# Moving twelve bias additions from GpSimd to VectorE in a four-layer graph network, and reordering the end of its third layer

## The chip, the cores and the metric

The kernel runs on one NeuronCore of a Trainium2 chip. A core has a matrix engine (PE, with PEld for its weight loads), a vector engine (DVE), an activation engine (ACT), a general-purpose engine (POOL, GpSimd) and a synchronising engine (SP) that here only starts DMA transfers. The engines run at the same time and wait for each other through semaphores. The metric is the device time of one execution in microseconds (us), as the median of several runs; lower is better.

## The reference, cut to what matters

Four graph layers follow each other on 512 nodes with 768 features; each adds its input and is normalised. All weights are 768 x 768 (or stacks of such).

```python
x = layernorm(x + L0(x))   # attention, 8 heads, then 1 head:  ... + b2
x = layernorm(x + L1(x))   # typed attention, twice:           ... + b2
x = layernorm(x + L2(x))   # three typed convolutions:         ... + b3
x = layernorm(x + L3(x))   # two plain convolutions:           ... + b2

# L2, one convolution (relu after the first two):
out = x @ root + bias
for r in range(4):                   # edge types
    out += rowscale_r * (C_r @ (x @ W[r]))
# L3: h = relu(A @ (x @ W1) + b1); out = A @ (h @ W2) + b2
```

So the last step of every layer is "input + bias row + aggregated products", and the kernel forms "input + bias row" ahead of time, in the buffer into which the products are then added. There are 16 such additions: four layers times four blocks of 128 nodes.

## The kernel before, in words

**Tiling.** Nodes are four blocks of 128 (NB = 4), features six chunks of 128 (KC = 6) or two halves of 384 (j = 0, 1). A product with a 768 x 768 weight is cut into two "units", one per half of the output columns; there are 78 units in the order of use (the list `weights`, then `units`). To keep float32 accuracy in a fast matrix format, every unit is held as three "forms" (w0, w1, w2) and the node matrix as three forms in the tiles S[0..2] (s): `split_piece` makes a third of a unit's forms with one ACT instruction (L778) and two DVE instructions (L779, L780), 128 x 768 each; `split_nodes` transposes a node block on PE (L792) and writes its three forms with ACT (L797) and DVE (L801, L802). The form buffers hold two units, so the forms of unit u go where unit u - 2 was.

**A product** (`product`) is four groups, one per node block: 12 matmuls with the first two forms (L821, L822), a scaling of the sums in PSUM by ACT (L823), then, one group later, 6 matmuls with the third form (L828) and the evacuation. After each group come a job from the list `between` and a call of `split_piece`. `close_group` issues what is open of the last group.

**Layer 0's end.** The last head's `aggregate` makes six columns of Y: PE L1176, then ACT L1183 and L1186, DVE L1187 and L1189, then the three forms of Y by ACT L1193 and DVE L1194 and L1195. The product `head.second` reads Y, with eight jobs that work out the last attention weights. The tiles xin (the layer's input) are loaded by SP (L1397) into buffers that the last head's rows leave free, and POOL adds the bias row (L1398).

**Layer 2, third convolution** (i = 3). Its input S is written column by column by the second convolution's `agg_columns`: DVE L2049, L2050, ACT L1980, DVE L1981, L1982. The output is summed up in acc (128 x 4 x 768), which is first loaded with layer 2's input (`residual`: SP L1989) and gets the bias row from POOL (L1990). Then come the products with root (two), the eight products with W[r] (c_p), and after each the aggregation of the one before it, `agg_rows`: 8 matmuls (L1931) and a DVE addition into acc (L2040). Sums into acc have no order of their own, except that all come after the load and the bias.

**The end of layer 2.** After the last product, six aggregations are left: blocks 2 and 3 of the first half (`agg_rows(R4 - 1, 0, b)`) and four blocks of the second half (`second(b)`). `norm` is DVE bn_stats (L890) twice, aggregate (L892), ACT square root (L894), DVE reciprocal (L895), and DVE subtract-and-scale (L896). `end2(b)` is norm, a store of the block to x_store[2], and `split_nodes` for layer 3. `end_of` puts end2(0) ahead after second(1); second(3) and the other three ends are jobs of layer 3's first product (d1_p0).

**Layer 3.** Two products with W1 (d_p), aggregation by columns (L1943), two with W2, aggregation into acc (L1931, L2114), norm and the output. Before the second product acc is loaded again from x_store[2] (L1989) and POOL adds the bias (L1990).

**What sets the order of instructions.** The code's order gives each instruction a priority; the framework's planner simulates the engines and gives each free engine the ready instruction with the highest priority, so that an instruction written later can be placed earlier when its engine would stand idle. `ahead(f, ...)` raises the priority by 100 places. On the chip each engine then runs its own list strictly in that order.

Of the kernel before, what the change touches and what calls it, by code (L numbers as in the profile page):

```python
# [8 lines left out]
F32 = mybir.dt.float32  # L9
# [13 lines left out]
P = 128  # L23
# [11 lines left out]
def gnn_stack_kernel(ctx: ExitStack, tc: tile.TileContext, a: dict, out: bass.AP):  # L35
# [121 lines left out]
    cT_store = dram.tile([R4 + 1, P, NB, N], F32, tag="cT", name="cT_store")  # L157
    packed_store = dram.tile([NB, P, N], I32, tag="packed", name="packed_store")
    log3_store = dram.tile([NB, P, R3, N], F32, tag="log3", name="log3_store")
    x_store = dram.tile([3, NB, P, D], F32, tag="x", name="x_store")  # L160
    key_store = dram.tile([R3, H1 * N], F32, tag="key", name="key_store")
    flag = const.tile([1, 1], I32, tag="flag", name="flag")

# [550 lines left out]
    def split_layers():  # L714
# [15 lines left out]
            weights += [a[f"L1_gnn_W{i}"][r] for r in range(R3)]  # L730
        for i in (1, 2, 3):
            these = [a[f"L2_gnn_W{i}"][r] for r in range(R4)]
            these.insert(i == 1, a[f"L2_gnn_root{i}"])
            weights += these
        weights += [a["L3_gnn_W1"], a["L3_gnn_W2"]]
        units = [
# [13 lines left out]
        raw, forms = {}, {}  # L750
        loaded, taken, cut, used = [0], [0], [0], [0]
        only_read = []

        def split_piece():

            if taken[0] == len(stream):
                return
            u, p, is_cut = stream[taken[0]]

            if is_cut and u > used[0]:  # L760
                return
            while loaded[0] < min(taken[0] + AHEAD + 1, len(stream)):
                at = loaded[0]
                v, q, _ = stream[at]
                raw[at] = raws.tile([P, KP, HD], F32, tag="raw", name=f"raw{at}")
                nc.sync.dma_start(raw[at], units[v][:, q * KP : (q + 1) * KP, :])
                loaded[0] += 1
            w = raw.pop(taken[0])
            taken[0] += 1
            if not is_cut:  # L770
                only_read[0](u - LAST0, p, w)
                return
            if p == 0:
                forms[u] = [
                    wforms.tile([P, KC, HD], F32R, tag=f"w{f}", name=f"w{f}_{u}") for f in range(3)
                ]
            hm, lo, df = (t[:, p * KP : (p + 1) * KP, :] for t in forms[u])
            nc.scalar.mul(hm, w, ROUND / SPLIT)  # L778
            nc.vector.scalar_tensor_tensor(lo, hm, -SPLIT, w, op0=ALU.mult, op1=ALU.add)  # L779
            nc.vector.tensor_sub(df, hm, lo)  # L780
            cut[0] += 1
# [50 lines left out]

            open_group.append(rest)

        def product(left, evac, name, between=()):

            w = next_unit()
            for b in range(NB):
                bs = slice(b * P, (b + 1) * P)
                po = bank(f"{name}_{b}")  # L840
                group(
                    po[:, :HD],
                    lambda f, bs=bs: [(left[f][:, k, bs], w[f][:, k, :]) for k in range(KC)],
                    lambda b=b, po=po: evac(b, po),
                )
                for job in between[b : b + 1]:
                    job()
                split_piece()

        def product_columns(left, j, evac, name, between=()):  # L850

# [135 lines left out]
        with (  # L987
# [361 lines left out]
            for i in range(H0):  # L1349
                head.aggregate()  # L1350
                jobs = []
                if i == 0:
                    after.h = [row_tile(f"{after.name}_h{b}") for b in range(NB)]
                    for fill in late:
                        fill()
                    after.project(halves=(1,), late=None)
                elif i + 1 < H0:
                    after = Head(i + 1)
                    more = []
                    if i < 3:  # L1360
                        first = 2 * (i - 1)
                        more = [lambda: None] * 8
                        more[1] = lambda: decode3(first)
                        more[5] = lambda: decode3(first + 1)
                    elif i == 3:
                        more = [
                            lambda: None, check_counts, lambda: degrees(0), lambda: None,
                            lambda: None, lambda: degrees(1),
                        ]
                    elif i == 4:  # L1370
                        more = [lambda: None] * 8
                        more[2], more[5] = lambda: degrees(2), lambda: degrees(3)
                    after.project(more)
                if i + 1 < H0:
                    w = after.w
                    soft = [lambda b=b, w=w: w.soft(b) for b in range(NB)]
                    turn = [lambda b=b, w=w: w.turn(b) for b in range(NB)]
                    jobs = [
                        lambda: None, w.keys, soft[0], soft[1], soft[2],
                        lambda: (soft[3](), turn[0]()), lambda: turn[1](),  # L1380
                        lambda: (turn[2](), turn[3]()),
                    ]
                else:
                    cols = small.tile([P, 2, NB], F32, tag="cols", name="gl_cols")
                    w = Weights(cols, "gl")

                    def last_scores():
                        rows = work.tile([P, N], F32, tag="elu_e", name="gl_rows")[:2, :]
                        early.first_rows(Y)
                        early.last_rows(Y, rows)  # L1390
                        nc.vector.tensor_add(cols, parts, early.columns())

                    brow = row_on_all(work, a["L0_gnn_b2"], "gl_b", "arow")
                    xin = []
                    for b in range(NB):
                        xin.append(row_tile(f"xin0_{b}"))
                        nc.sync.dma_start(xin[b], a["x"][b * P : (b + 1) * P, :])  # L1397
                        nc.gpsimd.tensor_tensor(xin[b], xin[b], brow, op=ALU.add)  # L1398
                    soft = [lambda b=b: w.soft(b, divide=False) for b in range(NB)]
                    turn = [lambda b=b: w.turn(b) for b in range(NB)]  # L1400
                    jobs = [
                        last_scores, w.keys, *soft, lambda: turn[0](),
                        lambda: (turn[1](), turn[2](), turn[3]()),
                    ]
                head.second(jobs)
                close_group()
                if i + 1 < H0:
                    head = after
# [575 lines left out]
        def bias_row(v, name):  # L1984
            return row_on_all(tail, v, name, "brow")

        def residual(x_of, b, brow):

            nc.sync.dma_start(acc[:, b, :], x_of)  # L1989
            nc.gpsimd.tensor_tensor(acc[:, b, :], acc[:, b, :], brow, op=ALU.add)  # L1990

        def end_of(second, end):


            second(0)
            second(1)
            ahead(end, 0)
            second(2)
            return [
                lambda: (second(3), ahead(end, 1)), lambda: ahead(end, 2), lambda: ahead(end, 3)  # L2000
            ]


        for i in (1, 2, 3):
# [7 lines left out]
            if i == 3:  # L2012
                brow = bias_row(a["L2_gnn_b3"], f"{name}_b")
                for b in range(NB):
                    residual(x_store[1, b], b, brow)
            def roots(i=i, name=name):
                for j in range(2):

# [11 lines left out]
                    else:  # L2030
                        product_columns(S, j, keep_columns, f"{name}_root{j}")

            if i > 1:
                roots()
            hs = {}

# [18 lines left out]
            for at, (r, j) in enumerate(order):  # L2055
                h = hs[r, j] = new_h(f"{name}_h{r}_{j}")
                jobs = ()
                if j == 0 and r < 2 or j == 1 and 1 <= r < R4 - 1:
                    to = r if j == 0 else r + 1
                    fetch(to)  # L2060
                    if i == 1:
# [2 lines left out]
                                rdeg_row[:, to, :], rdeg[:, to, :], f"rdeg{to}"  # L2064
                            )
                        ]
                if i == 3 and (r, j) == order[-1]:
                    jobs = [lambda: None, lambda: None, lambda: agg_rows(r, 0, 0), lambda: agg_rows(r, 0, 1)]
                if i == 1 and at == 0:
# [2 lines left out]
                    continue  # L2072
                if i == 1 and at == 1:
                    jobs = first_jobs
                product(S, lambda b, po, h=h: split_h(h, b, po), f"{name}_p{r}_{j}", jobs)
                if i == 1 and at == 1:
                    roots()
                if 0 < at and (i < 3 or at < len(order) - 1):
                    close_group()
# [6 lines left out]
            if i < 3:  # L2086
                agg_columns(*order[-1])
                continue
            agg_rows(R4 - 1, 0, 2)
            agg_rows(R4 - 1, 0, 3)  # L2090

            def end2(b):
                norm(acc[:, b, :], b, "l2")
                nc.sync.dma_start(x_store[2, b], acc[:, b, :])
                split_nodes(acc[:, b, :], b, "c3")

            late_ends = end_of(lambda b: agg_rows(R4 - 1, 1, b), end2)


        cT = new_c("d_cT")  # L2100
        nc.gpsimd.dma_start(cT, cT_store[R4])
        row_on_all_of(dinv_row, dinv, "dinv")
        for i in (1, 2):
            name = f"d{i}"
            hs = {}
            if i == 2:
                brow = bias_row(a["L3_gnn_b2"], f"{name}_b")
                for b in range(NB):
                    residual(x_store[2, b], b, brow)

            def agg(j, b):
                po = aggregate(cT, hs[j], b, f"{name}_a{j}")
                half = acc[:, b, columns_of(j)]
# [4 lines left out]
            for j in range(2):  # L2118
                h = hs[j] = new_h(f"{name}_h{j}")
                jobs = ()  # L2120
                if i == 1 and j == 0:
                    jobs = late_ends
                elif i == 2 and j == 1:
                    jobs = [lambda: None, lambda: None, lambda: agg(0, 0), lambda: agg(0, 1)]
                product(
# [66 lines left out]
```

## Time and profile before

| | us |
|---|---|
| median of three runs | 1650.72 (1647.27 to 1652.73) |
| the profiled execution | 1655.17 |
| its span, first to last instruction | 1653.4 |
| PE busy | 1590.9 (96%) |
| DVE busy | 1203.9 (73%) |
| ACT busy | 785.3 (47%) |
| POOL busy | 57.8 (3%), of it 31.4 for the 16 bias additions (8.3, 8.4, 7.4 and 7.3) |

Everything that the prediction takes from the trace is in microseconds from the span's start. In a timeline row the columns are start, duration, engine, line, operation, what is written and read, shapes and number of instructions; in brackets stands how long the engine stood idle before it, and what ended that. Matmuls overlap, so a row's duration is longer than the distance to the next one. In a table by stretches each engine has its busy time and its number of instructions, and PEclk is the share of the full TensorE clock that was granted. The layers lie at about 0 to 694 (layer 0), to 1047 (layer 1), to 1579 (layer 2) and to the end (layer 3).

### The profile page before, as it was taken

How to read it: one execution, taken by the hardware profiler on the slowest of the kernel's cores; microseconds unless marked ns; L12 is line 12 of the kernel's file. 1: busy time of each engine (PE TensorE's matmuls, PEld its weight loads, DVE VectorE, ACT ScalarE, POOL GpSimd, SP SyncE). 2: the span in 40 equal slices, each digit the busy share in tenths (PEclk: the TensorE clock that was granted, in tenths of full speed). 3: DMA queues.
4: the chain of work that ended last, by engine and by line, in shares of the span. 5: the costliest groups of instructions: out<-in, count | busy, mean ns of one | idle time of the engine just before them, and what ended most of it. 6: DMA issues, size and time to landing. Idle time of an engine off the chain costs nothing.

```text
span 1653.4 us, 21322 instructions
## 1 busy us (share of the span) xinstructions
PE 1590.9 (96%) x8085; PEld 1365.7 (83%) x8085; DVE 1203.9 (73%) x2154; ACT 785.3 (47%) x1350; POOL 57.8 (3%) x76
## 2 busy tenths in 40 slices
PE   5989999999999998999899999999999999999997
PEld 2759788797969786776789986889989998999887
DVE  8978898888979697645785986456665568644684
ACT  5665655654555554333785472343344333333352
POOL 0000000000000001000001000000000002000010
PEclk8999999999999999999999999999999999999999
DMA  3233233223323122232113363323332234332321
GB/s 125 78 121 97 89 105 99 86 90 89 106 78 114 38 87 77 97 112 87 45 40 133 97 193 122 116 79 102 96 105 86 83 102 142 101 93 83 112 77 40
DMA packets 84941, 158.04 MB, mean 96 GB/s; under 512 B 6176, under 2 KB 67992, under 8 KB 83168
## 3 DMA queue, kind: packets, MB, share of 16 engines
q1 hardware_dynamic: 79072, 127.79, 25.1%
q0 software_dynamic: 4544, 25.60, 4.7%
q10 hardware_dynamic: 1216, 3.22, 0.5%
q8 instruction: 65, 1.06, 0.3%
q14 instruction: 44, 0.36, 0.1%
HBM read 139.79 MB, written 16.79 MB: 95 GB/s over the span
## 4 chain that ended last, share of the span: by engine, by line
PE 76%; DVE 14%; ACT 4%; DMA 3%; issue 2%; ACTq 0%; DVEq 0%; SPq 0%
PE g_o L1176 10%; PE c_p L821 6%; PE c_p L822 6%; PE c_p L828 6%; PE c_a L1943 5%; PE r_o L1856 4%; PE g_s L821 3%; PE g_s L822 3%; PE g_s L828 3%; PE g_p L821 3%; PE g_p L822 3%; PE g_p L828 2%; PE c_a L1931 2%; PE r_p L821 2%; PE r_p L822 2%
## 5 line engine op out<-in xcount | busy, mean ns | idle before, releaser
L779 DVE SCALAR_TENSOR_TENSOR w<-w,raw 128x768 fp32r<-128x768 f32 x234 | 226.3, 971 | 115.0 <-ACT w L778 112.6
L778 ACT ACTIVATE w<-raw 128x768 fp32r<-128x768 f32 x234 | 195.5, 840 | 126.5 <-PE c_p L821 35.8
L780 DVE TENSOR_TENSOR w<-w,w 128x768 fp32r<-128x768 f32 x234 | 219.0, 951 | 10.4 <-PE c_root L828 4.4
L821 PE MATMUL c_p<-w,s 128*128 128x384 f32 x576 | 192.8, 335 | 0.0
L822 PE MATMUL c_p<-w,s 128*128 128x384 f32 x576 | 192.4, 334 | 0.0
L1176 PE MATMUL g_o<-wT,g_h 128*128 128x512 f32 x384 | 167.0, 595 | 2.6 <-ACT wT L1132 2.6
L1176 PEld LDWEIGHTS g_o<-wT,g_h 128*128 128x128 f32 x384 | 72.7, 191 | 92.3 <-issue 86.4
L1918 DVE TENSOR_TENSOR c_h_lo<-c_p,c_h_hi 128x384 fp32r<-128x384 f32 x96 | 53.2, 554 | 124.1 <-ACT c_h_hi L1917 124.1
L823 ACT ACTIVATE c_p<-c_p 128x384 f32<-128x384 f32 x96 | 45.5, 474 | 196.0 <-PE c_p L822 195.9
L821 PE MATMUL g_s<-w,y 128*128 128x384 f32 x384 | 131.9, 343 | 3.2 <-ACT y L1193 3.2
L821 PE MATMUL g_p<-w,s 128*128 128x384 f32 x384 | 135.0, 351 | 0.0
L822 PE MATMUL g_s<-w,y 128*128 128x384 f32 x384 | 129.3, 337 | 1.0 <-DVE y L1194 1.0
L822 PE MATMUL g_p<-w,s 128*128 128x384 f32 x384 | 130.1, 339 | 0.1
L828 PE MATMUL c_p<-w,s 128*128 128x384 f32 x576 | 117.5, 338 | 0.0
L822 PEld LDWEIGHTS c_p<-w,s 128*128 128x128 f32 x576 | 108.1, 188 | 0.8
L821 PEld LDWEIGHTS c_p<-w,s 128*128 128x128 f32 x576 | 108.1, 188 | 0.7
L828 PEld LDWEIGHTS c_p<-w,s 128*128 128x128 f32 x576 | 100.2, 188 | 4.1 <-ACT c_p L823 4.0
L828 PE MATMUL g_p<-w,s 128*128 128x384 f32 x384 | 79.3, 340 | 0.4 <-ACT g_p L823 0.3
L828 PE MATMUL g_s<-w,y 128*128 128x384 f32 x384 | 78.7, 340 | 0.3 <-ACT g_s L823 0.3
L821 PEld LDWEIGHTS g_s<-w,y 128*128 128x128 f32 x384 | 72.4, 188 | 4.2 <-ACT y L1193 4.0
L822 PEld LDWEIGHTS g_p<-w,s 128*128 128x128 f32 x384 | 72.6, 189 | 3.2 <-issue 1.9
L821 PEld LDWEIGHTS g_p<-w,s 128*128 128x128 f32 x384 | 72.6, 189 | 3.1 <-issue 2.0
(336 smaller groups left out, 3321.1 us busy)
## 6 DMA issues: line engine op xcount, KB each, us to landing
raw<-in_L_gnn_W_dram SPq DMA_DIRECT2D x222, 384.0 KB
c_cT<-cT_store POOLq DMA_DIRECT2D x12, 1024.0 KB, 5.9
raw<-in_L_gnn_root_dram SPq DMA_DIRECT2D x18, 384.0 KB
r_log<-log_store SPq DMA_DIRECT2D x8, 768.0 KB
cT_store<-r_qk SPq DMA_DIRECT2D x20, 256.0 KB
g_s<-in_L_gnn_a_src_dram POOLq DMA_DIRECT2D x8, 384.0 KB, 4.2
g_d<-in_L_gnn_a_dst_dram POOLq DMA_DIRECT2D x8, 384.0 KB, 4.4
log_store<-z SPq DMA_DIRECT2D x12, 256.0 KB
```

Source lines behind the costliest of these rows:

```text
L778: nc.scalar.mul(hm, w, ROUND / SPLIT)
L779: nc.vector.scalar_tensor_tensor(lo, hm, -SPLIT, w, op0=ALU.mult, op1=ALU.add)
L780: nc.vector.tensor_sub(df, hm, lo)
L821: nc.tensor.matmul(out, l0, r0, start=(k == 0), stop=False)
L822: nc.tensor.matmul(out, l1, r1, start=False, stop=(k == KC - 1))
L823: nc.scalar.mul(out, out, SPLIT + 1.0)
L828: nc.tensor.matmul(out, l2, r2, start=False, stop=(k == KC - 1), skip_group_check=True)
L1176: nc.tensor.matmul(po, self.h[k][:, c * P : (c + 1) * P], wT[:, k, :], start=(k == 0), stop=(k == NB - 1),)
L1856: nc.tensor.matmul(po[:, :n], wT[:, k, :], source(k, at), start=(k == 0), stop=(k == NK - 1),)
L1918: nc.vector.tensor_sub(lo, po[:, :HD], hi)
L1931: nc.tensor.matmul(po[:, :HD], cT[:, k, bs], h[f][:, k, :], start=(k + f == 0), stop=(k == NB - 1 and f == 1),)
L1943: nc.tensor.matmul(po, h[f][:, k, cs], cT[:, k, :], start=(k + f == 0), stop=(k == NB - 1 and f == 1),)
```

## The change

1. Layer 0: the four POOL additions into xin become DVE additions, two in each of the last two jobs of `head.second`.
2. Layer 2, third convolution: the four POOL additions into acc become DVE additions, jobs of the first product. The products with root move behind the first two products with W[0]; the list of weights is changed accordingly.
3. Layer 3: x_store[2], its four stores and four loads go away. The normalised blocks stay in acc, and the bias is added there by DVE, as jobs of the second product with W1.
4. The end of layer 2: the order is now sum, sum, ..., all six aggregations, with the four norms and the transposes of the first two blocks put between or behind them; the transposes of the last two blocks are jobs of layer 3's first product.
5. The last product of layer 2 no longer calls `split_piece` (unit 74, W1's first half, is cut at the start of its own product in the code's order), and unit 75 (W1's second half) first gets a copy of one column of S from the third block into its first form: its forms can't be made before that block's S is written.

The four additions in layer 1 (L1849) stay on POOL.

```diff
-        x_store = dram.tile([3, NB, P, D], ...)
+        x_store = dram.tile([2, NB, P, D], ...)
...
-            these.insert(i == 1, a[f"L2_gnn_root{i}"])
+            these.insert(i != 2, a[f"L2_gnn_root{i}"])
...
+        behind = {len(units) - 3: lambda: S[2][:, KC - 1, 3 * P - 1 : 3 * P]}
...
+            if p == 0 and u in behind:
+                nc.scalar.copy(hm[:, 0, :1], behind[u]())
             nc.scalar.mul(hm, w, ROUND / SPLIT)
...
-        def product(left, evac, name, between=()):
+        def product(left, evac, name, between=(), cuts=True):
...
-                split_piece()
+                if cuts:
+                    split_piece()
...
-                        nc.gpsimd.tensor_tensor(xin[b], xin[b], brow, op=ALU.add)
+                    def bias(*blocks):
+                        for b in blocks:
+                            nc.vector.tensor_add(xin[b], xin[b], brow)
...
-                        last_scores, w.keys, *soft, lambda: turn[0](),
-                        lambda: (turn[1](), turn[2](), turn[3]()),
+                        last_scores, w.keys, *soft, lambda: (turn[0](), bias(0, 1)),
+                        lambda: (turn[1](), turn[2](), turn[3](), bias(2, 3)),
...
-        def residual(x_of, b, brow):
-            nc.sync.dma_start(acc[:, b, :], x_of)
-            nc.gpsimd.tensor_tensor(acc[:, b, :], acc[:, b, :], brow, op=ALU.add)
-        def end_of(second, end):
+        def add_bias(b, brow):
+            nc.vector.tensor_add(acc[:, b, :], acc[:, b, :], brow)
+        def end_of(first, second, rows, turn):
+            first(2)
             second(0)
+            first(3)
             second(1)
-            ahead(end, 0)
+            ahead(rows, 0)
             second(2)
-            return [
-                lambda: (second(3), ahead(end, 1)), lambda: ahead(end, 2), lambda: ahead(end, 3)
-            ]
+            ahead(rows, 1)
+            ahead(second, 3)
+            ahead(turn, 0)
+            ahead(rows, 2)
+            ahead(turn, 1)
+            ahead(rows, 3)
+            return [lambda: ahead(turn, 2), lambda: ahead(turn, 3)]
...
-                    residual(x_store[1, b], b, brow)
+                    nc.sync.dma_start(acc[:, b, :], x_store[1, b])
...
-            if i > 1:
+            if i == 2:
                 roots()
...
+                if i == 3 and at == 0:
+                    jobs = [lambda b=b, brow=brow: add_bias(b, brow) for b in range(NB)]
...
-                product(S, lambda b, po, h=h: split_h(h, b, po), f"{name}_p{r}_{j}", jobs)
-                if i == 1 and at == 1:
+                product(
+                    S, lambda b, po, h=h: split_h(h, b, po), f"{name}_p{r}_{j}", jobs,
+                    cuts=i < 3 or at < len(order) - 1,
+                )
+                if i != 2 and at == 1:
                     roots()
...
-            def end2(b):
-                norm(acc[:, b, :], b, "l2")
-                nc.sync.dma_start(x_store[2, b], acc[:, b, :])
-                split_nodes(acc[:, b, :], b, "c3")
-            late_ends = end_of(lambda b: agg_rows(R4 - 1, 1, b), end2)
+            late_ends = end_of(
+                lambda b: agg_rows(R4 - 1, 0, b), lambda b: agg_rows(R4 - 1, 1, b),
+                lambda b: norm(acc[:, b, :], b, "l2"),
+                lambda b: split_nodes(acc[:, b, :], b, "c3"),
+            )
...
+        brow = bias_row(a["L3_gnn_b2"], "d_b")
...
-            if i == 2:
-                brow = bias_row(a["L3_gnn_b2"], f"{name}_b")
-                for b in range(NB):
-                    residual(x_store[2, b], b, brow)
...
+                elif i == 1:
+                    jobs = [lambda b=b: add_bias(b, brow) for b in range(NB)]
```

More of the change, by code (lines that the diff above doesn't have):

```diff
@@ L159, in gnn_stack_kernel @@
     log3_store = dram.tile([NB, P, R3, N], F32, tag="log3", name="log3_store")
-    x_store = dram.tile([3, NB, P, D], F32, tag="x", name="x_store")
+    x_store = dram.tile([2, NB, P, D], F32, tag="x", name="x_store")
     key_store = dram.tile([R3, H1 * N], F32, tag="key", name="key_store")
@@ L2088, in split_layers @@
                 continue
-            agg_rows(R4 - 1, 0, 2)
-            agg_rows(R4 - 1, 0, 3)
-            def end2(b):
-                norm(acc[:, b, :], b, "l2")
-                nc.sync.dma_start(x_store[2, b], acc[:, b, :])
-                split_nodes(acc[:, b, :], b, "c3")
-            late_ends = end_of(lambda b: agg_rows(R4 - 1, 1, b), end2)
+            late_ends = end_of(
[3 more added lines that the diff above has]
+            )
         cT = new_c("d_cT")
```

## The prediction

> **What bounds the kernel now.** I read the page's busy shares and its chain first: PE is busy for 96% of the span and has 76% of the chain, so an edit elsewhere pays only where PE stands still. Then I listed PE's idle stretches in the timeline. Between 560 and 1653 us, outside layer 1, only three places have idle rows over 0.15 us on PE: layer 0's end, the start of layer 2's third convolution, and layer 2's end. The change touches exactly these.
>
> Layer 0's end, PE, then POOL, then DVE:
>
> ```profile
> 630.04 0.44 PE L822 MATMUL g_s<-w,y 128*128 128x384 f32 x1 [0.75 <-DVE y L1194]
> 635.57 0.44 PE L821 MATMUL g_s<-w,y 128*128 128x384 f32 x1 [3.22 <-ACT y L1193]
> ...
> 627.60 8.25 POOL L1398 TENSOR_TENSOR xin<-xin,gl_b 128x768 f32<-128x768 f32 x4 [42.58 <-DMA xin<-in_x_dram]
> ...
> 624.24 0.68 DVE L1195 SCALAR_TENSOR_TENSOR y<-y,y 128x512 fp32r<-128x512 f32 x1
> 628.36 1.63 DVE L1194 TENSOR_TENSOR y<-g_y,y 128x512 fp32r<-128x512 f32 x1 [1.04 <-ACT y L1193]
> 629.91 2.06 DVE L1187 TENSOR_SCALAR g_e<-g_e 128x512 f32<-128x512 f32 x1
> 631.89 2.29 DVE L1195 SCALAR_TENSOR_TENSOR y<-y,y 128x512 fp32r<-128x512 f32 x1
> ```
>
> While POOL adds, three DVE instructions take 1.63, 2.06 and 2.29 us; the same lines take 0.69, 0.42 and 0.68 just before. PE waits behind them. The start of the third convolution shows the same: two S forms at 1.75 and 2.37 instead of 0.68, each beside a POOL addition.
>
> ```profile
> 1389.57 2.06 POOL L1990 TENSOR_TENSOR acc<-acc,c_b 128x768 f32<-128x768 f32 x1 [0.46 <-DMA acc<-x_store]
> ...
> 1390.42 1.75 DVE L1981 SCALAR_TENSOR_TENSOR s<-acc,s 128x512 fp32r<-128x512 f32 x1
> 1392.70 2.37 DVE L1982 SCALAR_TENSOR_TENSOR s<-s,s 128x512 fp32r<-128x512 f32 x1
> ...
> 1396.32 0.79 PE L822 MATMUL c_root<-w,s 128*128 128x384 f32 x3 [1.14 <-DVE s L1981]
> ```
>
> Layer 2's end: PE waits for the norms, DVE is full (11.77 of 12.00 us in 1553 to 1565), and weight forms stand between the norms.
>
> ```profile
> 1561.67 1.19 PE L792 MATMUL c_t<-ident,acc 128*128 128x128 f32 x6 [3.04 <-DVE acc L896]
> 1578.83 0.84 PE L792 MATMUL c_t<-ident,acc 128*128 128x128 f32 x6 [1.56 <-DVE acc L896]
> ...
> 1559.60 0.90 DVE L779 SCALAR_TENSOR_TENSOR w<-w,raw 128x768 fp32r<-128x768 f32 x1
> 1576.59 2.09 DVE L896 TENSOR_SCALAR acc<-acc,l_mv,l_rstd 128x768 f32<-128x768 f32 x1
> ...
> 1549.46 0.85 ACT L778 ACTIVATE w<-raw 128x768 fp32r<-128x768 f32 x1 [2.82 <-PE c_p L821]
> ...
> 636.00:642.00 6.00, 5.31 (x20) 2.60 (x18) 1.52 (x3) 1.49 (x3) 0.00 (x0) 0.72 0.00 0
> 1562.00:1582.00 20.00, 18.02 (x103) 16.98 (x101) 16.14 (x31) 7.11 (x17) 5.55 (x3) 0.91 0.45 155
> ```
>
> The last two rows are stretches: the granted clock is 0.72 and 0.91 right behind the two long waits. After 3.04 us of idle time the matmuls at 1562.5 come every 0.32 us instead of 0.173. So a long wait costs its length and a slow stretch after it.
>
> **Layer 0's end.** Idle: 0.75 + 3.22 + 0.22 + 0.33 = 4.5 us. Slow stretch, by the distances of matmuls at full clock: 12 matmuls in 1.11, 2.26 and 0.83 us instead of 0.52, 1.37 and 0.52, so 1.8. Ceiling 6.3. Without POOL the three DVE instructions lose 0.94 + 1.64 + 1.62 = 4.2 us, so the last column's forms come 4.2 us earlier, at about 631.4 and 632.2. PE then has its 8 matmuls of 0.25 us up to 631.2 and waits some 0.2 twice: no slow stretch. The four additions on DVE cost 0.87 each, by L780, which has the same shape, both inputs in SBUF, and that distance: 3.5 us. They are written into the last jobs, 655 to 666, where DVE is busy 18.4 of 25 us and PE is never idle: free there. But they are ready when the loads land, near 628 to 635, and the planner may put one into a pause of DVE on the chain (there are two, of 1.0 and 0.7 us). All four there would cost 3.5 and leave 0.7. I take **5.0** (between 0.7 and 6.3, near the top since whatever else waits on DVE has the higher priority).
>
> **Start of the third convolution.** PE needs 10.3 us for the 59 matmuls between 1388.12 and 1400.65 and takes 12.5: 2.25 lost. The two slow forms cost DVE 1.07 + 1.69 = 2.8 us, which is more, so nearly all goes. Worst: all four additions (3.5) between S's columns, 0.7 slower than now. DVE's list is full up to 1399 with work of higher priority, so I take **1.8** (-0.7 to 2.25). Behind it, four DVE additions may stand waiting for loads that land as late as 1402.2; queued behind them are forms of the product after next and evacuations, both a product (12.5 us) early: nothing. Moving root by two products adds no PE instruction, and the h tiles that then wait longest are not needed earlier: nothing; its other side is a stall of DVE of at most those 3 us, under the same 12.5.
>
> **Layer 2's end.** Between 1558.30 and 1582.54 PE has 80 matmuls and 28 transposes, 16.9 us at full distances, and takes 24.2: 7.3 lost, of it 5.0 idle (3.04, 0.41, 1.56) and 2.3 slow. After the change all six sums stand before the first transposes: 6 x 1.39 us from 1552.9, up to 1561.2. The first norm needs its sum (done by 1557.1 at the latest), then 2.7 us of DVE and ACT: ready at 1559.8, before PE has run out. What is late next is DVE: from 1553.3 it has six additions (3.1), seven bn_stats (3.3), norms (2.8), two blocks of S forms (3.8) and an h form (0.5), so 13.5 us, until about 1566.7, while PE wants the second block's forms near 1565.5. With unit 75's six instructions (5.2 us) still in between, that would be 5 us later; this is what the copy prevents. I leave 2.5 us of waits, with no slow stretch: gain **4.8** (top 7.3). The held forms become due at about 1576, when PE starts W1's second half; DVE can begin them at 1569.7, behind 1.9 us for the fourth block and 1.5 for h forms, so the first pieces are there and the last comes about on time. The copy itself is one small ACT instruction, nearest row L894 (128x1, 0.29 us), with scalings (L823) queued behind it; between 0 and 1 us, inside the 2.5.
>
> **Layer 3.** Four stores and four loads go from SP's queue; nobody on PE waits for them. The load of layer 3's bias row (0.55 on POOL) is written earlier, behind the load of its matrix; POOL has nothing else queued until the end, and now it runs at 1405, some 170 us early: nothing. Root's weight loads swap places with W[0]'s in SP's list, as many and as large: nothing. POOL's additions at 1568 to 1588 go, and with them the two slow norms (1.55 and 2.09 against 0.67), already counted. The four DVE additions (3.5) fall into 1577 to 1597, where DVE has 14.7 of 20 us and PE is dense; should they slip into the columns after it (DVE 14.56 of 16) they delay S by up to 0.9 each. I take **-0.4** (0 to -3.5).
>
> Sum: 5.0 + 1.8 + 4.8 - 0.4 = **11.2 us** off the profiled execution's 1655.17 (span 1653.4 and 1.8 around it), so 1644.0. The median shown is 4.45 lower; the edits have nothing to do with that difference, so the forecast is 1650.72 - 11.2 = **1639.5**.
>
> The Trainium skill speaks against a part of this. "TensorE: Matmul & The Clock Gate", in Part 1, has the clock halved only after an idle window of about 3.4 us. By it neither wait here (3.04, 3.22) would bring a slow stretch, and 4.1 us of the ceilings would not exist: about 7 us instead of 11.2. The rows of 0.72 and 0.91 show that they did.
>
> **Rivals.** (a) *One site does not pay*: the xin additions land in the chain of Y, leaving 0.7 of 5.0, or DVE remains the bound at layer 2's end, leaving about 0.5 of 4.8. Sum near 6.9, time 1644 (1642 to 1647.5). For it: DVE is full there whatever POOL does. Against: the weight forms leave. 20%. (b) *No change*: POOL isn't the cause of the slow instructions, or PE's waits only move; 1650. Against it: every slow instruction lies beside a POOL addition, in all three places. 11%. (c) *Slower*: W1's forms come too late. Unit 74 is no longer cut in the last product but behind the norms in priority. If its six DVE instructions (5.2 us) really come after 1553, DVE has 16.2 + 5.2 us until 1574.5 before layer 3's first group can end; PE is out of work at 1564.5, idles 10 us, runs 2.3 slow, and with layer 3's four additions (3.5) in the same queue and 1 us for unit 75 loses 16.8 instead of 7.3. That is 9.5 worse against 6.8 gained elsewhere: 1653.5. It decides when the three ACT instructions of unit 74 start after 1553. Against it: now they start at 1529.82, as soon as the buffer is free and 8 us ahead of their place in the code, as do those of every unit before it. 9%.
>
> **Numbers.** The main case has 60%: 1634.8 (all ceilings) to 1642. About 0.3% (5 us) is what a measurement of this kernel can tell from no change, so faster means under 1645.8: all of the main case and 13 of (a)'s 20 points, 73%. Within: 7 of (a), 10 of (b), 1 of (c), 18%. Slower: 8 of (c), 1 of (b). The range from 1634 to 1650 holds the main case, (a) and half of (b).
>
> **What would show it.** Right: in the changed trace L1194, L1187 and L1195 take 0.4 to 0.7 us at 627 to 632 and PE idles under 1 us there; no S form over 1 us at the third convolution's start; the last sum before the first L792 of layer 3, idle time before that under 1 us; L778 of unit 75 after 1565; granted clock 1.00 in both stretches. Wrong: DVE additions within the chain of Y, or PE idle ahead of W1's products.

## The result and the profile after

The changed kernel takes 1640.90 us (median of 7 runs, 1638.24 to 1642.83); the kernel before, on the same chip, 1650.72 (7 runs, 1646.32 to 1652.73). The ratio is 0.9942, 95% interval 0.993 to 0.9953. The forecast of 1639.5 was 1.4 us low. The profiled execution took 1640.9 us with a span of 1639.1. One execution in experiment 9 took 2282.56 us at a mean granted clock of 0.66 and is left out of that experiment's ratio.

In the changed file the prediction's lines have moved. L1187, L1189, L1193, L1194 and L1195 are now L1194, L1196, L1200, L1201 and L1202; L778 to L780 are L783 to L785; L792 is L797; L821, L822, L823 and L828 are L826, L827, L828 and L833; L896 is L903; L1931 is L1942; L1981, L1982, L2040 and L2049 are L1992, L1993, L2058 and L2067. New are the additions (L1408 in layer 0, L2000 in layers 2 and 3) and the copy (L782). In the kernels of experiments 2, 3 and 11 some lines move on by one to six more.

I cut both traces at the same instructions and compared the stages. Outside the three places all engines have the same lists of instructions.

| stage, cut at | before | after | difference |
|---|---|---|---|
| start, to the issue of the bias row gl_b | 584.49 | 583.29 | -1.20, same list |
| layer 0's end, to layer 1's first load on POOL | 110.77 | 105.20 | -5.57 |
| layer 1 | 352.12 | 350.11 | -2.01, same list |
| layer 2's first two convolutions | 341.19 | 341.22 | +0.03, same list |
| third convolution's first relation | 76.57 | 74.32 | -2.25 |
| its other relations | 72.95 | 73.01 | +0.06, same list |
| layer 2's end, to layer 3's first aggregation | 57.63 | 54.21 | -3.42 |
| the rest | 57.68 | 57.74 | +0.06 |

The touched stages gained 11.2 us. The spans differ by 14.3 because untouched code was 3.1 faster in this one execution; the medians differ by 9.8.

**Layer 0's end after**, timeline of DVE and PE, then one stretch (columns: stretch, its length, busy time of PE, PEld, DVE, ACT and POOL, granted clock, DMA):

```profile
626.38 0.96 DVE L1408 TENSOR_TENSOR xin<-xin,gl_b 128x768 f32<-128x768 f32 x1 [0.26 <-DMA xin<-in_x_dram]
627.26 0.68 DVE L1201 TENSOR_TENSOR y<-g_y,y 128x512 fp32r<-128x512 f32 x1
627.86 0.42 DVE L1194 TENSOR_SCALAR g_e<-g_e 128x512 f32<-128x512 f32 x1
628.20 0.68 DVE L1202 SCALAR_TENSOR_TENSOR y<-y,y 128x512 fp32r<-128x512 f32 x1
...
632.07 0.80 PE L833 MATMUL g_s<-w,y 128*128 128x384 f32 x3 [0.34 <-ACT g_s L828]
...
632.00:638.00 6.00, 5.79 (x33) 4.56 (x34) 2.06 (x4) 1.39 (x4) 0.00 (x0) 1.00 0.01 3
```

The three slow instructions are at 0.68, 0.42 and 0.68 us. PE's waits for Y (0.75, 3.22 and 0.22 us) are gone; the 0.34 us left are the wait for ACT's scaling that was there before (0.33). The clock stays at 1.00 where it was 0.72. One of the new additions stands at 626.38, in the middle of Y's chain; the other three followed at 629.46, 630.93 and 632.40.

**The third convolution's start after**, DVE, then the stretch:

```profile
1385.87 0.94 DVE L2000 TENSOR_TENSOR acc<-acc,c_b 128x768 f32<-128x768 f32 x1
1386.73 0.68 DVE L1992 SCALAR_TENSOR_TENSOR s<-acc,s 128x512 fp32r<-128x512 f32 x1
...
1388.20 0.68 DVE L1993 SCALAR_TENSOR_TENSOR s<-s,s 128x512 fp32r<-128x512 f32 x1
...
1386.00:1398.00 12.00, 11.99 (x69) 11.66 (x68) 11.61 (x16) 6.95 (x15) 0.54 (x1) 1.00 0.45 130
```

The S forms take 0.68 us although additions stand between them, and PE is busy for 11.99 of 12 us. In the 12.53 us from 1379.37, which match the prediction's 1388.12 to 1400.65, it is busy for 12.52 us (10.90 before).

**Layer 2's end after**, PE, then ACT, then stretches:

```profile
1550.32 0.82 PE L797 MATMUL c_t<-ident,acc 128*128 128x128 f32 x6
1553.30 1.54 PE L797 MATMUL c_t<-ident,acc 128*128 128x128 f32 x6 [2.17 <-DVE acc L903]
...
1538.52 0.85 ACT L783 ACTIVATE w<-raw 128x768 fp32r<-128x768 f32 x1 [2.82 <-PE c_p L826]
1539.69 0.82 ACT L783 ACTIVATE w<-raw 128x768 fp32r<-128x768 f32 x1
1560.28 0.18 ACT L782 CAST w<-s 128x1 fp32r<-128x1 f32 x1
1562.18 0.84 ACT L783 ACTIVATE w<-raw 128x768 fp32r<-128x768 f32 x1
...
1552.00:1558.00 6.00, 4.70 (x24) 4.63 (x25) 5.66 (x16) 2.96 (x7) 0.00 (x0) 0.72 0.00 0
1562.00:1582.00 20.00, 20.00 (x116) 19.70 (x115) 14.71 (x19) 10.52 (x19) 0.00 (x0) 1.00 0.25 79
```

All six sums now stand ahead of the first transposes, which start at 1550.32 without a wait. The second block's transposes still wait 2.17 us for their norm, and the six transposes take 1.54 us instead of 0.82: a slow stretch. From 1562 on PE is full (20.00 of 20). The ACT rows hold the surprise. The copy (1560.28) and the form behind it (1562.18) came late as wanted, but two thirds of unit 75 (1538.52, 1539.69) went ahead of the norms all the same. The copy is written for p == 0 alone, and it touches one column of the first third; the other two thirds depend on nothing.

### The profile page after: what moved, and what is told of

Its sections match the earlier page's. It is cut to its first block, busy times and chain, and to the rows that moved or that the text cites. A ratio compares the mean times of both kernels' runs of the same rounds, so it can differ in the third digit from the quotient of the medians.

```text
span 1639.1 us, 21279 instructions
## 1 busy us (share of the span) xinstructions
PE 1587.8 (97%) x8085; PEld 1366.4 (83%) x8085; DVE 1199.1 (73%) x2166; ACT 785.9 (48%) x1351; POOL 33.7 (2%) x64
## 3 DMA queue, kind: packets, MB, share of 16 engines
q10 hardware_dynamic: 1216, 3.22, 0.5%
## 4 chain that ended last, share of the span: by engine, by line
PE 83%; DVE 10%; ACT 4%; DMA 2%; issue 1%; ACTq 0%; DVEq 0%
PE g_o L1183 10%; PE c_p L833 6%; PE c_p L826 6%; PE c_p L827 6%; PE c_a L1954 5%; PE r_o L1867 4%; PE g_s L826 3%; PE g_s L827 3%; PE g_s L833 3%; PE g_p L826 3%; PE g_p L827 3%; PE r_p L826 3%; PE r_p L827 3%; PE r_p L833 3%; PE g_p L833 3%; PE c_a L1942 2%
## 5 line engine op out<-in xcount | busy, mean ns | idle before, releaser
L784 DVE SCALAR_TENSOR_TENSOR w<-w,raw 128x768 fp32r<-128x768 f32 x234 | 222.0, 953 | 114.3 <-ACT w L783 112.4
L783 ACT ACTIVATE w<-raw 128x768 fp32r<-128x768 f32 x234 | 195.3, 839 | 126.4 <-PE c_p L826 35.9
L785 DVE TENSOR_TENSOR w<-w,w 128x768 fp32r<-128x768 f32 x234 | 218.8, 950 | 10.5 <-PE c_root L833 4.4
L826 PE MATMUL c_p<-w,s 128*128 128x384 f32 x576 | 191.2, 335 | 0.0
L827 PE MATMUL c_p<-w,s 128*128 128x384 f32 x576 | 190.8, 334 | 0.0
L828 ACT ACTIVATE c_p<-c_p 128x384 f32<-128x384 f32 x96 | 45.3, 474 | 191.8 <-PE c_p L827 191.8
L826 PE MATMUL g_p<-w,s 128*128 128x384 f32 x384 | 134.6, 351 | 0.0
L826 PE MATMUL g_s<-w,y 128*128 128x384 f32 x384 | 131.9, 343 | 0.0
L827 PE MATMUL g_p<-w,s 128*128 128x384 f32 x384 | 130.1, 339 | 0.1
L827 PE MATMUL g_s<-w,y 128*128 128x384 f32 x384 | 129.3, 337 | 0.1
L833 PE MATMUL c_p<-w,s 128*128 128x384 f32 x576 | 117.3, 338 | 0.0
L827 PEld LDWEIGHTS c_p<-w,s 128*128 128x128 f32 x576 | 108.0, 188 | 0.8
L826 PEld LDWEIGHTS c_p<-w,s 128*128 128x128 f32 x576 | 108.0, 188 | 0.7
L833 PEld LDWEIGHTS c_p<-w,s 128*128 128x128 f32 x576 | 100.2, 188 | 4.2 <-ACT c_p L828 4.2
L833 PE MATMUL g_p<-w,s 128*128 128x384 f32 x384 | 79.3, 340 | 0.4 <-ACT g_p L828 0.3
L833 PE MATMUL g_s<-w,y 128*128 128x384 f32 x384 | 78.1, 338 | 0.3 <-ACT g_s L828 0.3
L827 PEld LDWEIGHTS g_p<-w,s 128*128 128x128 f32 x384 | 72.6, 189 | 3.1 <-issue 1.9
L1954 PE MATMUL c_a<-c_cT,c_h_lo 128*128 128x512 f32 x192 | 75.1, 391 | 0.0
L1954 PE MATMUL c_a<-c_cT,c_h_hi 128*128 128x512 f32 x192 | 75.1, 391 | 0.0
```

What stands on the lines that cost most here:

```text
L826: nc.tensor.matmul(out, l0, r0, start=(k == 0), stop=False)
L827: nc.tensor.matmul(out, l1, r1, start=False, stop=(k == KC - 1))
L828: nc.scalar.mul(out, out, SPLIT + 1.0)
L833: nc.tensor.matmul(out, l2, r2, start=False, stop=(k == KC - 1), skip_group_check=True)
L1954: nc.tensor.matmul(po, h[f][:, k, cs], cT[:, k, :], start=(k + f == 0), stop=(k == NB - 1 and f == 1),)
```

## The experiments

My theory after reading the traces had three parts. First, DVE instructions are slow only beside POOL's additions, by contention and not by a dependency. Second, layer 2's end gained from POOL, from the order and from the held form, each in part. Third, it gained less than forecast because two thirds of unit 75 were not held. The rivals are in the expectations. Each kernel below is the changed kernel with the edit shown; its stage times stand against the changed kernel's 105.20, 74.32 and 54.21 us.

### 1. Layer 0's additions on POOL again

```diff
-                            nc.vector.tensor_add(xin[b], xin[b], brow)
+                            nc.gpsimd.tensor_tensor(xin[b], xin[b], brow, op=ALU.add)
```

> The changed kernel with one thing undone: layer 0's four additions stand on POOL again, in the old place of the code. Contention theory: DVE's instructions become slow only beside POOL's additions. L1201, L1194 and L1202 beside them take 1.6 to 2.3 us again, PE waits 0.8 and 3.2 us, the stretch behind it runs at a granted clock near 0.72, and layer 0's end takes 5.6 us more than in the changed kernel; the other two places stay as in the changed kernel; the time is about 1646.5. Rival, order: the gain came from the additions' place among DVE's instructions or from run-to-run differences in untouched code; then the three instructions keep 0.4 to 0.7 us and layer 0's end takes 0 to 1 us more, time about 1641.

Measured: 1645.76 us (8 runs), ratio to before 0.9967 (0.9957 to 0.9978). Layer 0's end takes 110.36 us, 5.16 more; the other two places are as in the changed kernel (74.32, 54.17). POOL, DVE and PE:

```profile
625.59 1.84 POOL L1408 TENSOR_TENSOR xin<-xin,gl_b 128x768 f32<-128x768 f32 x1 [42.64 <-DMA xin<-in_x_dram]
627.61 6.23 POOL L1408 TENSOR_TENSOR xin<-xin,gl_b 128x768 f32<-128x768 f32 x3 [0.18 <-DMA xin<-in_x_dram]
...
626.28 1.70 DVE L1201 TENSOR_TENSOR y<-g_y,y 128x512 fp32r<-128x512 f32 x1 [1.04 <-ACT y L1200]
627.90 2.06 DVE L1194 TENSOR_SCALAR g_e<-g_e 128x512 f32<-128x512 f32 x1
629.88 2.30 DVE L1202 SCALAR_TENSOR_TENSOR y<-y,y 128x512 fp32r<-128x512 f32 x1
632.10 0.74 DVE L1196 SCALAR_TENSOR_TENSOR g_y<-g_o,bcols,g_e 128x512 f32<-128x512 f32 x1
...
633.55 0.61 PE L826 MATMUL g_s<-w,y 128*128 128x384 f32 x1 [3.22 <-ACT y L1200]
```

The contention theory holds, with almost the old numbers: L1201, L1194 and L1202 take 1.70, 2.06 and 2.30 us, and PE waits 0.82 and 3.22 us; the granted clock from 634 to 640 is 0.74. Read L1201's end: 626.28 + 1.70 = 627.98. POOL's first addition ended at 627.43, 0.55 us earlier. L1196 at 632.10 also lies beside POOL's additions (627.61 to 633.84) and keeps its 0.74; its first input, g_o, comes from PSUM.

### 2 and 3. Work on POOL that nobody waits for

Four extra additions on POOL, each started by the landing of a block of x, and in a second kernel three memsets in the place of each addition:

```diff
+                    spare = work.tile([P, D], F32, tag="arow", name="spare")
+                    for b in range(NB):
+                        nc.gpsimd.tensor_copy(spare[:, :1], xin[b][:, :1])
+                        nc.gpsimd.tensor_tensor(spare, brow, brow, op=ALU.add)
...
+                        for n in range(3):
+                            nc.gpsimd.memset(spare, float(n))
```

> The changed kernel with four extra POOL additions at layer 0's end whose result nobody uses, each with two inputs in SBUF (the bias row added to itself) and started by the landing of a block of x, as the old additions were; the four real additions stay on DVE. Contention theory: nobody waits for POOL's work, yet the DVE instructions beside it take 1.6 to 2.3 us, and layer 0's end is 4 to 5.6 us longer, or more, since the real additions on DVE become slow too. Rival, dependency: Y's chain was late because something waited for POOL's results or its queue; then nothing waits here and the stage is as long as in the changed kernel (0 to 0.3 us).

> The same place and trigger as the run with extra POOL additions, but POOL only writes: three memsets of 128x768 for each block of x, whose result nobody uses. If contention is a matter of POOL's use of SBUF as such, DVE's instructions beside the memsets are slow here as well (1.6 to 2.3 us, stage 3 to 6 us longer). If it takes POOL's reading of two inputs, they keep 0.4 to 0.7 us and the stage is as in the changed kernel (0 to 0.5 us). I expect the second, with 60 in 100.

Measured: with the extra additions layer 0's end takes 109.72 us (+4.52; one run, 1645.29), with the memsets 105.08 (-0.12; one run, 1642.39). POOL and DVE with the extra additions:

```profile
624.34 2.23 POOL L1409 TENSOR_TENSOR spare<-gl_b 128x768 f32<-128x768 f32 x1
627.24 1.54 POOL L1409 TENSOR_TENSOR spare<-gl_b 128x768 f32<-128x768 f32 x1
...
625.16 1.96 DVE L1201 TENSOR_TENSOR y<-g_y,y 128x512 fp32r<-128x512 f32 x1
627.38 1.95 DVE L1202 SCALAR_TENSOR_TENSOR y<-y,y 128x512 fp32r<-128x512 f32 x1
```

With the memsets:

```profile
628.38 2.55 POOL L1410 MEMSET spare<- 128x768 f32 x3
...
629.23 0.69 DVE L1201 TENSOR_TENSOR y<-g_y,y 128x512 fp32r<-128x512 f32 x1
629.84 0.42 DVE L1194 TENSOR_SCALAR g_e<-g_e 128x512 f32<-128x512 f32 x1
```

Nobody reads the spare tile, so nothing waits for the results of the extra additions. One dependency is left: DVE's addition into a block of x waits for POOL's one-column copy out of it (0.50 us before the first of them). The memset kernel has the same copies and loses nothing, so contention is shown. The size tells its kind. L1201 ends at 627.12 and POOL's addition at 626.57, 0.55 earlier; L1202 ends at 629.33 and POOL's next at 628.78, again 0.55. An instruction that takes 0.68 alone has 0.55 left when POOL's ends, whenever it started: it stands still until then. So DVE doesn't run at part speed, it waits. Beside memsets, which read nothing, DVE runs at its full speed.

"SBUF — State Buffer" in the Trainium skill, section "Who interferes with whom", states this as an exclusive lock: a DVE instruction with two SBUF inputs and a GpSimd instruction that reads SBUF can't run together, and the second one blocks fully. The rows agree: five ends at POOL's end plus 0.55 us (one in experiment 1, two here, two in experiment 11), none slow beside memsets.

### 4. No form held back

```diff
-        behind = {len(units) - 3: lambda: S[2][:, KC - 1, 3 * P - 1 : 3 * P]}
+        behind = {}
```

> The changed kernel without the held-back weight forms: no copy, unit 75's first third is made when its buffer is free, as the other two thirds already are in the changed kernel. As the prediction had it, the copy keeps 5.2 us of DVE work out of the norms: without it layer 2's end is 5 us longer, time about 1646. By the trace of the changed kernel only one third is held: 1.7 us of DVE work joins ahead of the norms, of which PE sees between 0 and 1.7 us: time 1641 to 1643. A third reading, that the copy does nothing: 0.

Measured: layer 2's end takes 55.12 us, 0.91 more; 1640.99 us (4 runs), ratio 0.994 (0.9923 to 0.9956), which the time can't tell from the changed kernel. PE waits 2.42 us ahead of the second block's transposes and 0.57 later. The prediction gave the copy 5 us; as written it is worth 0.9.

### 5 and 10. All of unit 75 held back

```diff
-            if p == 0 and u in behind:
+            if u in behind:
```

> The changed kernel with one more thing: the copy that holds a weight form back is written for all three thirds of unit 75, not for the first alone. My theory: in the changed kernel two thirds (3.6 us of DVE work) still go ahead of the norms, and turn 1 waits 2.17 us for its norm; with all of it held, norm 1 comes up to 2.2 us earlier, the wait is under 0.5 us, the clock stays at 1.00, and layer 2's end is 2 to 3.4 us shorter: time 1638 to 1639. Rival: DVE's order of sums, statistics and forms sets norm 1, not the weight forms; then the wait stays and the stage is as before (0 to 0.5 us). Second rival: with 5.2 us of forms behind the norms, W1's second half comes late; then PE waits ahead of its products at about 1573 and the time is 1641 to 1645.

> The changed kernel with all three thirds of unit 75 held back, timed in more rounds. Theory: the wait of turn 1 stays at 0.5 us, too short for a slow stretch, so layer 2's end is 51.8 us in every execution: 0.8 us less than the changed kernel where that one has no slow stretch, 2.4 less where it has one; median 1 to 2.4 us under the changed kernel's, ratio to before near 0.993. Rival: the gain of the profiled execution is given back in untouched code; then the two medians agree within 0.5 us.

Measured: layer 2's end takes 51.81 us in the first trace and 51.82 in the second, 2.4 less than in the changed kernel's profiled execution. Times: 1640.39 us (4 runs), ratio 0.9932 (0.9913 to 0.995), and 1639.95 (6 runs), ratio 0.993 (0.9916 to 0.9945). PE and ACT in the first trace:

```profile
1553.27 0.87 PE L797 MATMUL c_t<-ident,acc 128*128 128x128 f32 x6 [0.50 <-DVE acc L903]
...
1561.81 0.28 ACT L782 CAST w<-s 128x1 fp32r<-128x1 f32 x2 [1.02 <-DVE s L807]
1562.41 1.57 ACT L783 ACTIVATE w<-raw 128x768 fp32r<-128x768 f32 x2
1564.49 0.84 ACT L783 ACTIVATE w<-raw 128x768 fp32r<-128x768 f32 x1
```

Now all three forms start behind 1562, the wait for the norm is 0.50 us, the clock stays at 1.00, and no product of layer 3 waits for unit 75. The theory of the missing two thirds holds for the stage. That it shows in the time is likely, not certain: on the same chip as the second run the changed kernel's median was 1642.68 us, 2.7 more, and its ratio 0.994 (0.9923 to 0.9958), so the intervals overlap.

### 6. The old order at layer 2's end, additions on DVE

```diff
-            ahead(rows, 0)
+            ahead(end, 0)
             second(2)
-            ahead(rows, 1)
...
-            return [lambda: ahead(turn, 2), lambda: ahead(turn, 3)]
+            return [
+                lambda: (second(3), ahead(end, 1)), lambda: ahead(end, 2), lambda: ahead(end, 3)
+            ]
```

(with first(3) ahead of second(0) as before, and no form held back)

> The changed kernel, but at layer 2's end the old order of sums and transposes and no held-back form; layer 3's additions stay on DVE and the additions in place. It splits the gain of this stage (3.4 us) into the part of POOL's additions and the part of the order. Theory: the slow norms beside POOL's additions (1.55 and 2.09 instead of 0.67) were 2.3 us of the old stage, so it is 2 us shorter than before and 1.4 us longer than in the changed kernel, with waits ahead of the transposes of 2 to 3 us each still there: time about 1642. Rival: the order is all of it; then the stage is 3 us or more longer than in the changed kernel, 1644. Second rival: POOL is all of it; 0, 1641.

Measured: 56.54 us, 1.09 less than before and 2.33 more than in the changed kernel; 1642.55 us (4 runs), ratio 0.9947 (0.9928 to 0.9966). PE waits for the first block's norm as long as before the change:

```profile
1549.59 0.87 PE L797 MATMUL c_t<-ident,acc 128*128 128x128 f32 x6 [3.04 <-DVE acc L903]
```

So this stage's 3.42 us are 1.1 for the additions on DVE, in place and without the stores and loads, which no run takes apart (57.63 to 56.54), 1.4 for the order (to 55.12 in experiment 4) and 0.9 for the third that is held (to 54.21). All four kernels have one slow stretch here, so they can be compared. I had put POOL's part at 2.

### 7, 8 and 11. Root's place, cutting in the last product, POOL in the third convolution

```diff
-            these.insert(i != 2, a[f"L2_gnn_root{i}"])
+            these.insert(i == 1, a[f"L2_gnn_root{i}"])
...
-                    cuts=i < 3 or at < len(order) - 1,
+                    cuts=True,
...
                     nc.sync.dma_start(acc[:, b, :], x_store[1, b])
+                    nc.gpsimd.tensor_tensor(acc[:, b, :], acc[:, b, :], brow, op=ALU.add)
```

(three kernels; the first also calls roots() where it was called before, the third drops the DVE jobs)

> The changed kernel with the products of the third convolution's root ahead of the first relation's, as before; the additions stay on DVE. If the start of this convolution gained by POOL's silence alone, the stage behind it is as in the changed kernel (0 to 0.3 us). If the four additions on DVE then stand in the way of S's forms, up to 0.7 us of additions each, the stage is up to 2.8 us longer. I expect 0 to 1 us, since the acc of these additions is needed by root's sums first.

> The changed kernel, but the last product of layer 2 goes on cutting weight forms as before. In the changed kernel unit 74's forms were made in the same stretch as before, so the planner takes them when their buffer is free, wherever the code puts them; I expect 0 (within 0.3 us in layer 2's end). Rival: the order of writing counts for the planner's ties and the stage gets 1 to 3 us longer.

> The changed kernel with the third convolution's four additions on POOL again, right behind the loads of acc; root's products stay behind the first relation's. Contention theory: S forms beside POOL's additions take 1.7 to 2.4 us instead of 0.68, PE waits about 1.1 us and the stage is 1.5 to 2.3 us longer. Rival: what helped is that root's products come later, so that their additions are not due yet; then the S forms are slow or not, but PE doesn't wait: 0 to 0.3 us.

Measured, one run each (1637.82, 1640.41 and 1642.56 us). With root first the third convolution's first relation takes 74.26 us (-0.06): root's place is worth nothing once the additions are on DVE. With cuts=True the stages up to layer 2's end are as they were, and that end takes 52.58 instead of 54.21, with the same wait of 2.17 us and DVE's and ACT's instructions in the same order; experiment 9 shows why. With POOL's additions it takes 76.01 (+1.69), and the S forms are slow:

```profile
1382.23 2.07 POOL L2033 TENSOR_TENSOR acc<-acc,c_b 128x768 f32<-128x768 f32 x1 [0.46 <-DMA acc<-x_store]
...
1382.49 0.69 DVE L2068 TENSOR_TENSOR c_t<-c_a,rdeg_row 128x512 f32<-128x512 f32 x1
1383.09 1.76 DVE L1992 SCALAR_TENSOR_TENSOR s<-acc,s 128x512 fp32r<-128x512 f32 x1
```

L1992 (two inputs in SBUF) ends 0.55 us after POOL's addition: 1384.85 and 1384.30. L2068 (L2067 in the changed kernel), in the same 2 us, has one input in PSUM (c_a) and keeps its 0.69. A second pair is alike: L1992 ends at 1388.33, POOL's next addition at 1387.78. PE waits 0.49 and 0.55 us, where it was 0.48 and 1.14. The old place of root cost the other 0.6 us (76.57 against 76.01), so by these traces, one of each kernel, the place mattered only beside POOL.

### 9. The changed kernel again

> The changed kernel itself once more, on the same chip as the run that holds all of unit 75 back. Turn 1 waits 2.17 us in every trace of this code, and behind it the granted clock is 0.5 for 3.4 us in some traces and 1.00 in others; layer 2's end should be 54.2 us with the slow stretch or 52.6 without, nothing in between. Time 1639 to 1642.

Measured: ratio 0.994 (0.9923 to 0.9958). Its layer 2's end takes 54.19 us. The code of this end is the same, with the same 2.17 us wait, in eight traces of this study (cuts=True included, whose wait is the same). Five have 54.17 to 54.21 us (the changed kernel, 1, 2, 7, 9) and three 52.57 or 52.58 (3, 8, 11). The kernel with memsets has no slow stretch; PE, then the stretch:

```profile
1556.46 0.87 PE L797 MATMUL c_t<-ident,acc 128*128 128x128 f32 x6 [2.17 <-DVE acc L903]
...
1554.00:1560.00 6.00, 3.83 (x31) 3.55 (x30) 6.00 (x16) 3.49 (x9) 0.00 (x0) 1.00 0.00 0
```

Clock 1.00 here, 0.72 in the like stretch of the changed kernel, after an equal wait. One slow stretch costs 1.6 us of this stage.

## Why the prediction was right, point by point

**Layer 0's end: right.** Forecast -5.0 us; measured -5.57, and 5.16 by undoing it alone. The cause was named rightly. One step was wrong without cost: the additions did not run at 655 to 666. (The prediction's 18.4 of 25 us is not DVE's load there, which was 8.14 of 11; about as much, 18.27, lies in 641 to 666.) Three ran inside Y's chain and the fourth right behind it. The prediction had named this as a sign of being wrong and priced it at 3.5 us. Of the 2.6 us of the three, about 1.5 fell into pauses, by an estimate from DVE's idle rows (1.04 and 0.70 us in experiment 1, 0.26 here). The last forms started at 630.33 and 631.79, up to 0.8 us later than forecast when this trace's earlier start is allowed for, and PE waited for neither.

**The third convolution's start: right, small.** Forecast -1.8; measured -2.25, the ceiling. I had kept 0.45 for additions in the way of S. They do stand between S's last columns (1385.87), and PE doesn't notice. The loads came earlier than the 1402.2 that I had allowed for: all four additions are over by 1391.67.

**Layer 2's end: the direction right, a step wrong.** Forecast -4.8; measured -3.42. The step that failed is "with unit 75's six instructions (5.2 us) still in between, that would be 5 us later; this is what the copy prevents". The copy holds two of the six DVE instructions; the four others (3.5 us by the prediction's 0.87 each) ran ahead of the norms. I had read "p == 0" as "before the first piece, hence before all", though a dependency here joins only regions that overlap. Without the copy the stage is 0.9 us longer, not 5; with all three thirds held it is 2.4 shorter, in all 5.8 less than before. So all six instructions in between cost 3.3 us (51.81 to 55.12), a slow stretch included, and the 5 us were too much as well. "No slow stretch" failed with it: the wait left was 2.17 us, and 1.6 us of the stage hangs on the clock behind it. That DVE would be late next was right; it was late with the second block's norm, not with its S forms. The changed kernel without a slow stretch (52.6, -5.1) would have met the forecast, by luck.

**Layer 3 and the rest: right.** Forecast +0.4; measured +0.06. The additions run on DVE at 1565 to 1576 beside a full PE. The third rival (W1's forms late, slower) did not occur: unit 74's ACT instructions start at 1518.88, 8.3 us ahead of the stage's start, exactly as before (1529.82), and they do so with cuts=True too (experiment 8).

**The sum.** 11.2 us were forecast, and the three stages gave 11.2 in the profiled executions, partly by errors that cancel: 0.6 and 0.45 too little in the first two, 1.4 too much in the third, 0.3 too little in the rest. The medians gave 9.8 (7.8 to 11.6 by the interval) and the two spans 14.3, so untouched code moves a single time by more than the 1.4 us that the forecast missed by; that it came so close is in part luck. The part up to 584 us, untouched, took 579.4 to 585.0 us in this study's traces, and the granted clock from 10 to 580 us goes with it: 1.00 in the two fastest, 0.98 in the two slowest.

**The rule weighed.** "TensorE: Matmul & The Clock Gate", Part 1, made it about 7 us, since waits under 3.4 us should bring no slow stretch. The traces decide against that reading: after 2.17 us of idle time the clock was 0.5 in five of eight traces. The prediction's own case against the rule (3.04 and 3.22 us) holds as well. The same part also says that the window of 3413 ns is free-running. That fits the rest: the slow stretches lasted 3.4 us wherever I read both ends, and their start wandered against the wait. In the four traces with a wait of 2.17 us that I followed back, the 3.4 us before that start took in the whole wait; with the waits of 2.42 and 3.04 us (experiments 4 and 6) 2.0 and 2.5 us of it. That a wait counts when most of it falls into one window is inferred from this; no run here set the phase.

## What to carry to other kernels

Look for instructions of one engine that are longer than their own row elsewhere, and see what ran beside them. An addition moved off POOL is worth not its own time but the waits of the DVE chain beside it, and here it could be moved into that chain at no cost to PE, since the chain had pauses. When a false dependency is to hold work back, list every instruction of that work and see that each touches the region; then look in the next trace for the ones that went ahead.

## What the runs showed of the hardware

- A DVE instruction with two SBUF inputs stands still until POOL's addition has ended: it ended 0.55 us later in all five rows where it takes 0.68 alone. An input in PSUM freed it (0.74 and 0.69 beside POOL's additions), and memsets on POOL did not slow it (0.69 and 0.42).
- L1194, with one SBUF input, is held as well: 2.06 us instead of 0.42 beside POOL's additions, yet 0.42 beside POOL's memsets.
- A wait of 2.17 us on PE cost either itself (three traces) or itself and 1.6 us (five), with nothing in between, for the same instructions of this stage in the same order. No one kernel showed both. Waits of 0.5 us were followed by clock 1.00 in both traces that had them. So shortening the wait by 1.7 us was worth 2.4 us against the traces with a slow stretch and 0.8 against those without.
